# Cross-attention in float32: the tile of batch 0's first softmax sum, and the place of T4's copies on ScalarE in batches 2 to 5

## The chip, the cores and the metric

The kernel runs on one core of a Trainium2 chip. The core has TensorE (PE; its weight loads are listed apart as PEld), VectorE (DVE), ScalarE (ACT), GpSimd (POOL) and SyncE (SP). Each engine executes its own instructions in the order in which the program lists them; semaphores hold an instruction until the ones that it depends on are done. The metric is device time in microseconds. Before the change the median of three runs is 665.91 us (665.89 to 666.24).

## The reference

Eight batches of cross-attention with a residual, all in float32; x1 is `x` and x2 is `ctx_2048`, each 8 x 512 x 1024:

```python
q = jnp.einsum('bcn,dc->bnd', x1, Wq) + bq          # d = 64
k = jnp.einsum('bcn,dc->bdn', x2, Wk) + bk[:, None]
v = jnp.einsum('bcn,dc->bdn', x2, Wv) + bv[:, None]
attn = jax.nn.softmax(jnp.einsum('bnd,bdm->bnm', q, k), axis=2)
attn_out = jnp.einsum('bcm,bnm->bcn', v, attn)
return attn_out + x1
```

## The kernel before

One function, `period`, writes out the work of one batch `s` together with the early work of the next batches `n` and `nn`; it is called for the eight batches in turn, after `head` has begun batch 0. The order of every engine's instructions is the order of the calls in the code; nothing is rescheduled. The framework adds the waits.

**Scores.** For batch `n` the scores are made in two halves `h` of the queries (512 each) and four steps `i`. One step is a pair of score matmuls (L237), which run side by side into two PSUM banks, and two ScalarE copies (L246) into the tile e, one for each bank. In half 0 the banks come from a ring of four that is called `s`, but step 1 takes the two banks `c`. Step 3 of half 0 needs the banks of step 0. Behind the four steps TensorE projects the next batch's queries (L192): in batches 2 to 5 (`s.six`) into the next bank of the ring, which step 2 held; in the others into bank `c0`, which step 1 held. When that is done, SyncE loads the next x tile (L139).

**Softmax.** VectorE folds the maximum and the sum over the steps (`fold`, L258), GpSimd reduces them over the partitions (L274 for the maximum `top`, L306 for the sum `den`), VectorE subtracts the maximum (L342) and ScalarE takes the exponential (L351). `invert` sends the 512 reciprocals to a row in DRAM (L321), and `spread` reads it back onto all partitions (L327). The division comes later, on the product.

**Products.** x2 times the exponentials is computed before Wv is applied. Both are 2 x 2 block products by a seven-product scheme (Strassen's kind); most of the seven are split once more by the same scheme, into inner steps. The names are those of the scheme: product 6 multiplies `S2` and `T2`, product 4 multiplies a block with `T4`, and T4 = T2 - e21, where e21 is one block of the exponentials. `copy_t4` makes -e21 on ScalarE in two parts (L380, 128 x 1024 each), and `add_t4` has two GpSimd DMAs add T2 to it (L386). `multiply_seeded` runs the inner steps of one product in the order 1, 7, 6, 2, 5, 4, 3. Steps 1, 7, 6, 5 and 4 end in ScalarE copies (L858): step 7's goes into a tile v, the "third part", and the others into a bank of the product. Step 6 goes on in the bank `chain` that step 1 wrote, so it waits for step 1's copy. A hook can be hung behind a step.

**Batch 0** multiplies product 6 plainly (`parts_6`, L428) and copies it to the tile u6 on ScalarE (L441), just before the scores of batch 1. Its product 5 has its third part in a tile of the tag `r`.

**Tiles.** Tiles with the same tag share one piece of SBUF (here one buffer for each of `u6`, `r` and `eT4`). Whoever writes a new tile of a tag first waits until all readers of the tile before it are done. The sum of batch 0, half 0, is a tile of tag `u6`: it is folded on VectorE and reduced on GpSimd (L306), and after that u6 holds product 6. The two tags hold tiles of one size. T4's buffer holds, before T4, sums of product 2's inner steps.

Of the kernel before, what the change touches and what calls it, by code (L numbers as in the profile page):

```python
# [15 lines left out]
def kernel(  # L16
# [234 lines left out]
    def fold(s, h, i, kind, op):  # L251

        e = s.e[h]
        if i == 1:
            tag = "u6" if (kind, s.b, h) == ("sum", 0, 0) else "fold"
            s.mx[h] = sb.tile([P, 2, H], F32, tag=tag, name=f"{kind}_{s.b}_{h}")
        f = s.mx[h]
        nc.vector.tensor_tensor(f, e[:, :, 0, :] if i == 1 else f, e[:, :, i, :], op)  # L258

    def folds(s, h, kind, op, to=MH):  # L260

        for i in range(1, to):
            fold(s, h, i, kind, op)
            yield
# [109 lines left out]
    def copy_t4(s, parts=(0, 2)):  # L374

        if parts[0] == 0:
            s.t["T4"] = sb.tile([P, MH, H], F32, tag="eT4", name=f"eT4_{s.b}")
        t4 = s.t["T4"]
        for i in parts:
            nc.scalar.mul(t4[:, i : i + 2, :], s.t["21"][:, i : i + 2, :], -1.0)  # L380

    def add_t4(s):

        t4 = s.t["T4"]
        for i in (0, 2):
            nc.gpsimd.dma_start(t4[:, i : i + 2, :], s.t["T2"][:, i : i + 2, :], accum_op=ALU.add)  # L386
# [225 lines left out]
    def inner_product(s, i, z, ps, opens, *copies):  # L612

        ka, kb, _, _ = MULT[z]
        n_k = s.inner[i][ka].shape[1]
        for k in range(n_k):
            nc.tensor.matmul(  # L617
                ps,
                s.inner[i][ka][:, k, :],
                s.inner[i, "t"][kb][:, k, :],  # L620
                start=opens and k == 0,
                stop=z in (2, 3, 4) and k == n_k - 1,
                skip_group_check=True,
            )
        for copy in copies:
            nc.scalar.copy(copy, ps)

    def inner_parts(s, i):

        ks = ("third", "chain") if i in ((1, 6, 7) if s.six else (2, 7)) else ("chain", "third")  # L630
        of = {k: ps_s.tile([P, H], F32, tag="s", name=f"ps_i{i}{k}_{s.b}")[:, left] for k in ks}
        return of["chain"], of["third"]
# [202 lines left out]
    def multiply_seeded(s, i, v_tag, hooks={}, bank=None):  # L835

        bank = bank or MULT[i][2]

        def fresh(j):
            s.bank[bank, j] = ps = ps_a.tile(  # L840
                [P, H], F32, tag=f"{bank}{j}", name=f"ps_y{bank}{j}_{s.b}_{i}"
            )
            return ps

        b0 = fresh(0)
        chain, third = inner_parts(s, i)
        if v_tag == "top" or s.b == B - 1 and v_tag == "r":
            v = sb.tile([P, H], F32, tag="top", name=f"v{i}_{s.b}", bufs=2)[:, left]
        else:
            v = sb.tile([P, 2, H], F32, tag=v_tag, name=f"v{i}_{s.b}")[:, 0, left]  # L850
        seeded = s.six and i == 5
        if seeded:
            nc.scalar.copy(third, s.v6)

        def step(z, ps, opens, out=None, of=None):
            inner_product(s, i, z, ps, opens)
            if out is not None:
                nc.scalar.copy(out, of)  # L858
            if z in hooks:
                hooks[z]()  # L860

        step(1, chain, True, b0[:, left], chain)
        step(7, third, not seeded, v, third)
        if s.six and i == 6:
            s.v6 = v
        b1 = fresh(1)
        step(6, chain, False, b1[:, left], chain)
        step(2, b0[:, left], False)
        step(5, chain, False, b0[:, right], chain)
        step(4, b1[:, left], False, b1[:, right], chain)  # L870
        step(3, b0[:, right], False)

        def complete(b1=b1):
            b = b1.rearrange("p (a n) -> p a n", a=2)
            nc.vector.tensor_tensor(b, b, v.unsqueeze(1).to_broadcast([P, 2, H // 2]), ALU.add)

        return complete
# [211 lines left out]
    def sums(s, h):  # L1089
        for i in range(1, MH):  # L1090
            fold(s, h, i, "sum", ALU.add)
        total(s, h)
# [34 lines left out]
    def head(s):  # L1127
# [68 lines left out]
        for copy in copies:  # L1196
            copy()
        fold(s, 0, 1, "sum", ALU.add)
        fold(s, 0, 2, "sum", ALU.add)
        fold(s, 1, 1, "max", ALU.max)  # L1200
# [28 lines left out]
    def period(s, n, nn, nnn):  # L1229
# [4 lines left out]
        def first(i, rows=range(2)):  # L1234
            multiply(s, "y", i, s.a, s.t, MH, rows=rows)
# [119 lines left out]
        else:  # L1355
# [51 lines left out]
            if early:  # L1407
                invert(s, 0)
            if s.six:
                multiply_seeded(s, 6, "top", {6: lambda: copy_t4(s, (0,)), 4: lambda: copy_t4(s, (2,))})  # L1410
            else:
                if n:
                    copy_t4(s)
                    add_t4(s)
                first(6)
# [293 lines left out]
    with tc.manual_schedule():  # L1709
        head(states[0])  # L1710
        for b in range(B):
            period(*states[b : b + 4])
# [36 lines left out]
```

## Time and profile before

| | before |
|---|---|
| median of the runs | 665.91 us (665.89 to 666.24) |
| the profiled execution: its time / its span | 665.95 us / 664.2 us |
| TensorE busy | 658.2 us (99%) |
| weight loads busy | 437.4 us (66%) |
| VectorE busy | 622.9 us (94%) |
| ScalarE busy | 387.2 us (58%) |
| GpSimd busy | 215.5 us (32%) |
| granted TensorE clock | 1.0 |

The span is the time from the first to the last instruction of the program, and rows of the timeline give the start within the span, the duration, the engine, the line, the operation, out<-in, the shape and the count. A bracket at the end is idle time of that engine before the row, and what ended it. Where the wait was for several things, the profile names the one that it takes to have come last; if that one was done long before, it was another. A TensorE row's duration overlaps the next row's; distances between starts tell the pace. Float32 matmuls show as two records each. A busy TensorE is not one at its peak.

### The profile page before, as it was taken

The numbers are of one execution on the slowest core, as the hardware profiler recorded it, in microseconds if no ns is written. First come the engines' busy times: TensorE is split into PE (matmuls) and PEld (weight loads), VectorE is DVE, ScalarE is ACT, GpSimd is POOL, SyncE is SP. The second block draws the span as 40 slices with busy tenths as digits, with TensorE's granted clock in tenths as the row PEclk, the third lists the DMA queues.
The fourth block names the chain that finished last, engine by engine and source line by source line (L and its number), as shares of the span: only waits on it lengthen the run. The fifth ranks groups of instructions, "written<-read, shape, count | busy, mean of one in ns | idle before, by whom it ended". The sixth has DMA issues, their size and how long they took to land.

```text
span 664.2 us, 8111 instructions
## 1 busy us (share of the span) xinstructions
PE 658.2 (99%) x2644; PEld 437.4 (66%) x2644; DVE 622.9 (94%) x900; ACT 387.2 (58%) x744; POOL 215.5 (32%) x187
## 2 busy tenths in 40 slices
PE   9999999999999999999999999999999999999997
PEld 4434755757658666787667686676865757656865
DVE  1999999989999998999989999999989999999996
ACT  3754457546495666755667646766567456474332
POOL 0126115531237302282033820346212640224300
PEclk9999999999999999999999999999999999999999
DMA  8697578994789958999699996999957995368614
GB/s 334 252 269 242 139 242 151 215 250 157 234 177 218 244 189 283 175 191 255 183 283 186 191 270 191 250 204 183 292 145 141 207 207 175 76 130 181 121 41 150
DMA packets 48522, 133.26 MB, mean 201 GB/s; under 512 B 5600, under 2 KB 6112, under 8 KB 48480
## 3 DMA queue, kind: packets, MB, share of 16 engines
q0 software_dynamic: 21488, 59.32, 49.1%
q1 hardware_dynamic: 26848, 73.29, 30.5%
q8 instruction: 21, 0.34, 0.2%
q14 instruction: 21, 0.17, 0.1%
q10 hardware_dynamic: 144, 0.14, 0.1%
HBM read 87.83 MB, written 16.81 MB: 158 GB/s over the span
## 4 chain that ended last, share of the span: by engine, by line
PE 84%; DVE 10%; ACT 2%; DMA 1%; issue 1%; POOL 1%; SPq 0%; DVEq 0%
PE ps_yc L617 9%; PE ps_ya L617 7%; PE ps_oc L504 7%; PE ps_s L237 4%; PE ps_oa L504 4%; PE ps_q L192 3%; PE ps_i5chain L617 3%; PE ps_i7chain L617 3%; PE ps_k L192 3%; PE ps_ya L504 3%; PE ps_oa L801 3%; PE ps_i4b L952 3%; PE ps_i3chain L617 3%; PE ps_i1chain L617 3%; PE ps_i2chain L617 3%; PE ps_oc L952 2%
## 5 line engine op out<-in xcount | busy, mean ns | idle before, releaser
L342 DVE TENSOR_TENSOR e<-e,top 128x1024 f32<-128x1024 f32 x60 | 72.2, 1219 | 0.2 <-POOL top L274 0.2
L351 ACT ACTIVATE e<-e 128x1024 f32<-128x1024 f32 x60 | 62.9, 1061 | 15.6 <-DVE e L342 15.3
L274 POOL PARTITION_ALL_REDUCE top<-max x16 | 32.1, 2009 | 110.6 <-DVE max L268 51.7
L246 ACT COPY e<-ps_s 128x512 f32<-128x512 f32 x90 | 47.8, 623 | 9.7 <-PE ps_s L237 7.1
L237 PE MATMUL ps_s<-q,k 64*128 64x512 f32 (+1 forms) x188 | 47.4, 599 | 0.2 <-ACT e L246 0.2
L306 POOL PARTITION_ALL_REDUCE den<-sum x10 | 33.2, 3316 | 31.6 <-DVE sum L268 31.6
L258 DVE TENSOR_TENSOR max<-max,e 128x1024 f32<-128x1024 f32 x30 | 36.6, 1221 | 0.3
L237 PEld LDWEIGHTS ps_s<-q,k 64*128 64x128 f32 x188 | 17.6, 186 | 20.7 <-issue 16.5
L987 DVE TENSOR_TENSOR y<-y,den 128x1024 f32<-128x1024 f32 x24 | 29.3, 1223 | 0.3
L858 ACT COPY ps_yc<-ps_i7chain 128x256 f32<-128x256 f32 x32 | 11.4, 357 | 28.9 <-PE ps_i7chain L617 15.2
L569 DVE TENSOR_TENSOR aI<-a 128x256 f32<-128x256 f32 x60 | 26.8, 447 | 0.0
L287 POOL PARTITION_ALL_REDUCE den<-sum x6 | 19.4, 3230 | 22.0 <-DVE sum L268 22.0
L192 PE MATMUL ps_q<-x_in_x_dram,wqk_sb 128*64 128x512 f32 x112 | 25.6, 598 | 0.4
L327 POOL DMA_DIRECT2D den<-row x12 | 6.7, 560 | 57.8 <-DMA row<-few 42.7
L504 PE MATMUL ps_oc<-yT,w 128*128 128x512 f32 x56 | 25.3, 594 | 0.2 <-DVE uo L1051 0.2
L504 PE MATMUL ps_oa<-yT,w_S 128*128 128x512 f32 x56 | 25.2, 593 | 0.0
L858 ACT COPY ps_ya<-ps_i5chain 128x256 f32<-128x256 f32 x32 | 11.5, 361 | 21.6 <-PE ps_i5chain L617 17.3
L617 PE MATMUL ps_yc<-e,aI 128*128 128x256 f32 x92 | 23.6, 379 | 0.0
L258 DVE TENSOR_TENSOR max<-e 128x1024 f32<-128x1024 f32 x15 | 18.3, 1220 | 5.0 <-POOL den L306 3.1
L858 ACT COPY ps_ya<-ps_i1chain 128x256 f32<-128x256 f32 x28 | 10.0, 357 | 22.1 <-PE ps_i1chain L617 17.0
L170 POOL DMA_DIRECT2D aS<-in_x2T_dram x7 | 6.3, 897 | 50.1 <-ACT aS L166 50.1
L858 ACT COPY ps_yc<-ps_i3chain 128x256 f32<-128x256 f32 x32 | 11.4, 357 | 18.4 <-PE ps_i3chain L617 14.2
(395 smaller groups left out, 1913.8 us busy)
## 6 DMA issues: line engine op xcount, KB each, us to landing
x_in_x_dram<-in_x_dram SPq DMA_DIRECT2D x60, 512.0 KB, 7.7
a<-in_x2T_dram SPq DMA_DIRECT2D x32, 512.0 KB, 8.1
eT<-eT POOLq DMA_DIRECT2D x24, 512.0 KB, 8.4
aS<-in_x2T_dram POOLq DMA_DIRECT2D x21, 512.0 KB, 5.6
uo<-in_x_dram POOLq DMA_DIRECT2D x17, 512.0 KB, 10.7
e<-e POOLq DMA_DIRECT2D x13, 512.0 KB, 7.5
r<-in_x_dram POOLq DMA_DIRECT2D x11, 512.0 KB, 6.8
out_dram<-r SPq DMA_DIRECT2D x11, 512.0 KB, 3.7
```

The source lines that it names most:

```text
L192: nc.tensor.matmul(ps[r, :], w_sb[:, c, :], s.x[:, c, ts(h, H)], start=(c == 0), stop=(c == CT - 1),)
L237: nc.tensor.matmul(ps[g][:, n], s.k[r, ts(i, P)], s.q[r, ts(h, H)][:, n], start=True, stop=True)
L246: nc.scalar.copy(e[:, g, i, :], ps[g])
L258: nc.vector.tensor_tensor(f, e[:, :, 0, :] if i == 1 else f, e[:, :, i, :], op)
L274: nc.gpsimd.partition_all_reduce(s.top[h], s.mx[h][:, 0, :], P, ReduceOp.max)
L306: nc.gpsimd.partition_all_reduce(s.den[h], s.mx[h][:, 0, :], P, ReduceOp.add)
L342: nc.vector.tensor_tensor(e, e, top, ALU.subtract)
L351: nc.scalar.activation(e, e, AF.Exp)
L504: nc.tensor.matmul(ps, left[ka][:, k, ts(j, P)], right[kb][:, k, :], start=opens and k == 0, stop=i in (2, 3, 4) and k == n_k - 1, skip_gr ...
L617: nc.tensor.matmul(ps, s.inner[i][ka][:, k, :], s.inner[i, "t"][kb][:, k, :], start=opens and k == 0, stop=z in (2, 3, 4) and k == n_k - 1 ...
L858: nc.scalar.copy(out, of)
L952: nc.tensor.matmul(ps, s.inner[i][ka][:, k, :], s.inner[i, "t"][kb][:, k, :], start=opens and k == 0, stop=z in (2, 3, 4) and k == n_k - 1 ...
```

## The change

Two independent edits.

In `fold`, the sum of batch 0, half 0, takes the tag `r` instead of `u6`. In `period`, for batches 2 to 5, the first part of T4's copy is issued ahead of product 6 instead of behind its inner step 6, and the second part behind inner step 6 instead of behind step 4.

```diff
@@ fold
         if i == 1:
-            tag = "u6" if (kind, s.b, h) == ("sum", 0, 0) else "fold"
+            tag = "r" if (kind, s.b, h) == ("sum", 0, 0) else "fold"
             s.mx[h] = sb.tile([P, 2, H], F32, tag=tag, name=f"{kind}_{s.b}_{h}")
@@ period
             if s.six:
-                multiply_seeded(s, 6, "top", {6: lambda: copy_t4(s, (0,)), 4: lambda: copy_t4(s, (2,))})
+                copy_t4(s, (0,))
+                multiply_seeded(s, 6, "top", {6: lambda: copy_t4(s, (2,))})
```

The first edit moves no instruction; it changes what some wait for. ScalarE in batch 0, from T4's copies to the scores of batch 1 (`uy_0` is u6 with product 6, `e_0_405` the scores; `PE_49`, `Pool_49` and `DVE_49` are the engines' semaphores; - before, + after):

```order
 L380 ACTIVATE eT_0_327<-e_0_148 128x1024 x2
 L455 ACTIVATE k_359<-ps_k_358,wqk_sb 128x512 [waits PE_49]
-L441 COPY uy_0_378<-ps_ya_0_1_266 128x512 [waits PE_49,Pool_49]
+L441 COPY uy_0_378<-ps_ya_0_1_266 128x512 [waits PE_49]
 L441 COPY uy_0_378<-ps_ya_0_1_274 128x512 [waits PE_49]
-L246 COPY e_0_405<-ps_s_1_0_0_406 128x512 [waits PE_49]
+L246 COPY e_0_405<-ps_s_1_0_0_406 128x512 [waits DVE_49,PE_49]
 L246 COPY e_0_405<-ps_s_1_0_0_407 128x512 [waits PE_49]
 L246 COPY e_0_405<-ps_sc_1_0_1_412 128x512 [waits PE_49]
```

The product's first copy no longer waits for GpSimd; the first score copy now has a wait on VectorE of its own, for the last fold of the sum (L258). The wait on GpSimd goes to the copy of product 5's third part, the tile `v_0` of tag `r`, on ScalarE further on in batch 0:

```order
 L209 ACTIVATE q_439<-ps_q_430,wqk_sb 64x512
 L858 COPY ps_ya_0_5_463<-ps_i5chain_464 128x256 [waits PE_49,Activation_49]
-L858 COPY v_0_466<-ps_i5third_465 128x256 [waits PE_49]
+L858 COPY v_0_466<-ps_i5third_465 128x256 [waits PE_49,Pool_49]
 L858 COPY ps_ya_0_5_473<-ps_i5chain_464 128x256 [waits PE_49,Activation_49]
 L858 COPY ps_ya_0_5_463<-ps_i5chain_464 128x256 [waits PE_49]
```

Nothing else stands between them in another order. The second edit moves two rows on ScalarE. Batch 2, from the last copy of product 1 (L413) to the first score copy of batch 3; `eT` is T4, `ps_i6chain`, `ps_ya` and `v_2` are product 6's. Before:

```order
L413 COPY uy_2_1391<-ps_ya_2_1_1336 128x512
L858 COPY ps_ya_2_6_1414<-ps_i6chain_1416 128x256
L858 COPY v_2_1417<-ps_i6third_1415 128x256
L858 COPY ps_ya_2_6_1424<-ps_i6chain_1416 128x256
L380 ACTIVATE eT_2_1428<-e_0_919 128x1024
L858 COPY ps_ya_2_6_1414<-ps_i6chain_1416 128x256
L858 COPY ps_ya_2_6_1424<-ps_i6chain_1416 128x256
L380 ACTIVATE eT_2_1428<-e_0_919 128x1024
L246 COPY e_0_1451<-ps_s_3_0_0_1452 128x512
```

and after the change:

```order
L413 COPY uy_2_1391<-ps_ya_2_1_1336 128x512
L380 ACTIVATE eT_2_1414<-e_0_919 128x1024
L858 COPY ps_ya_2_6_1416<-ps_i6chain_1418 128x256
L858 COPY v_2_1419<-ps_i6third_1417 128x256
L858 COPY ps_ya_2_6_1426<-ps_i6chain_1418 128x256
L380 ACTIVATE eT_2_1414<-e_0_919 128x1024
L858 COPY ps_ya_2_6_1416<-ps_i6chain_1418 128x256
L858 COPY ps_ya_2_6_1426<-ps_i6chain_1418 128x256
L246 COPY e_0_1451<-ps_s_3_0_0_1452 128x512
```

Each of the two L380 rows stands three or two rows earlier, and nothing follows the last inner copy but the score copies. The first L380 keeps its waits, which are for the T4 transfers of the batch before. The second copy of product 6 to u6 (L408), behind the scores, gets a wait for ScalarE's own last inner copy. Batches 3 to 5 read the same, and the other engines' instructions stay in their order.

## The prediction

> **What bounds the kernel now.** I read the page first, then the chain that ended last, then who waited for whom, and last the timeline at the two edited places.
>
> ```profile
> PE 658.2 (99%) x2644; PEld 437.4 (66%) x2644; DVE 622.9 (94%) x900; ACT 387.2 (58%) x744; POOL 215.5 (32%) x187
> ```
>
> TensorE is busy for 658.2 of 664.2 us, and VectorE for 622.9. So an edit on ScalarE (ACT) or GpSimd (POOL) counts only where TensorE's work starts later because of it. Such a place stands in the chain, in batch 0:
>
> ```profile
> 50.87 3.24 POOL den L306
> 54.13 1.07 ACT uy L441 x2
> ...
> 55.74 1.61 PE ps_s L237 x3
> ```
>
> GpSimd reduces the first softmax sum, ScalarE waits for it to copy product 6 out, and TensorE's scores wait for ScalarE. The waits of ScalarE name the same place, and one that touches the second edit:
>
> ```profile
> ACT uy L441 <- POOL den L306: 4.5, 1, 4.5
> ...
> ACT e L246 <- ACT eT L380: 2.5, 4, 0.6
> ```
>
> The columns are total us, times, longest. The first is part 1 of the change. The second invites the reading that T4's copy (L380) keeps four batches' score copies waiting 0.6 us each; the timeline below decides that.
>
> **Part 1: the sum moves from tile u6 to tile r.** The copies at L441 write u6, which until now held the sum that the reduction L306 reads. With the sum in r, L441 waits only for its own matmuls. The same place before, on TensorE, ScalarE and the weight loads:
>
> ```profile
> 45.65 7.13 PE L428 MATMUL ps_ya<-eT,aS 128*128 128x512 f32 x16
> 52.72 1.13 PE L237 MATMUL ps_s<-q,k 64*128 64x512 f32 x4
> 55.09 1.09 ACT L246 COPY e<-ps_s 128x512 f32<-128x512 f32 x2
> 55.74 0.29 PEld L237 LDWEIGHTS ps_s<-q,k 64*128 64x128 f32 x2 [1.01 <-ACT e L246]
> 57.29 3.65 PE L192 MATMUL ps_q<-x_in_x_dram,wqk_sb 128*64 128x512 f32 x16
> ```
>
> Four pairs of score matmuls start at 52.72, the projection of the next queries at 57.29: 4.57 us. The fourth pair needs the banks of the first, which ScalarE frees late. The same sequence in batch 1, where nothing holds ScalarE:
>
> ```profile
> 135.45 1.13 PE L237 MATMUL ps_s<-q,k 64*128 64x512 f32 x4
> 136.65 1.07 ACT L246 COPY e<-ps_s 128x512 f32<-128x512 f32 x2 [0.51 <-PE ps_s L237]
> 139.08 1.51 PE L192 MATMUL ps_q<-x_in_x_dram,wqk_sb 128*64 128x512 f32 x6
> ```
>
> Here it takes 139.08 - 135.45 = 3.63 us, and the first copy starts 1.20 us after the first score. After the change the last product-6 matmul still ends at 45.65 + 7.13 = 52.78, the second L441 copy (1.07 / 2, about 0.55 us) ends near 53.4, and the first score copy starts at 52.72 + 1.20 = 53.92 in place of 55.09. That is soon enough for the fourth pair to find its banks free, so TensorE gains 4.57 - 3.63 = **0.94 us** at this place. The wait does not vanish: it goes to the copy of product 5's third part into r, at about 62 us, while the reduction ended at 50.87 + 3.24 = 54.11; cost nothing, with 8 us to spare. The first score copy also gets a wait for VectorE's last fold of the sum; in the chain the reduction that reads this sum starts at 50.87, so the fold was over before 52.72. No DMA moves past another.
>
> Does the 0.94 us reach the end? VectorE is not moved by it at first, and then meets two places where it waited for TensorE anyway:
>
> ```profile
> 67.44 1.23 DVE L599 TENSOR_TENSOR eI3eT<-e 128x1024 f32<-128x1024 f32 x1 [0.78 <-PE ps_ya L617]
> 73.00 0.70 DVE L875 TENSOR_TENSOR ps_yc<-ps_yc,v 128x512 f32<-128x512 f32 x1 [0.40 <-ACT ps_yc L858]
> 77.30 0.56 POOL L327 DMA_DIRECT2D den<-row  x1 [10.95 <-DMA row<-few]
> 77.88 1.78 POOL L274 PARTITION_ALL_REDUCE top<-max  x1
> 79.98 0.28 DVE L641 TENSOR_TENSOR w_I<-w,w_I 128x128 f32<-128x128 f32 x1
> 80.18 2.35 DVE L342 TENSOR_TENSOR e<-e,top 128x1024 f32<-128x1024 f32 x2
> ```
>
> It had 0.78 idle before 67.44 and 0.40 before 73.00, together 1.18, so from 73 on it is 0.94 earlier too. What is late next is GpSimd: its maximum (L274) stands behind the issue of L327, which waits for the 2 KB row of reciprocals. If that row lands no earlier, the maximum still ends at 77.88 + 1.78 = 79.66, and VectorE, which subtracts it from 80.18, gains at most 80.18 - 79.66 = 0.52. What the row stands behind:
>
> ```profile
> 60.98 1.75 SPq L139 DMA_DIRECT2D x_in_x_dram<-in_x_dram  x4
> 65.07 1.28 POOL L321 DMA_DIRECT2D row<-few  x1
> 62.00:66.00 4.00, 4.00 (x20) 3.23 (x19) 4.00 (x8) 1.76 (x5) 3.70 (x5) 1.00 0.87 318
> 66.00:70.00 4.00, 4.00 (x20) 3.53 (x19) 3.22 (x7) 1.15 (x4) 0.35 (x1) 1.00 0.92 271
> ```
>
> (The last two are stretches; the number before the last is the DMA engines' busy share.) SyncE's four x loads, issued when the query projection has freed x, fill the engines at 0.87 to 0.92, and GpSimd's two T4 transfers and the row follow. The loads' issue hangs on the projection and moves 0.94 earlier; in a queue this full most of that should reach the row. Bounds: the row moves by 0 or by 0.94. I take 0.94, since the queue is busy throughout. With 0 VectorE lags TensorE by 0.94 - 0.52 = 0.42, and the tightest place behind is
>
> ```profile
> 126.88 2.35 DVE L365 TENSOR_TENSOR eT<-eT,e 128x1024 f32<-128x1024 f32 x2
> 128.49 7.03 PE L504 MATMUL ps_ya<-eT,aS 128*128 128x512 f32 x16
> ```
>
> The first of the two sums ends about 126.88 + 1.2 = 128.1, 0.4 us before product 6 of batch 1 reads it, and the weight loads want it some 0.2 sooner. TensorE would lose 0.2 to 0.4 there, and part 1 would be worth 0.5 to 0.7.
>
> **Part 2: T4's copies one place forward, batches 2 to 5.** Per batch two ScalarE copies of 1.06 us, none added. The first moves from behind product 6's third step to ahead of its first; the second takes its place. In batch 2:
>
> ```profile
> 209.26 0.59 ACT L413 COPY uy<-ps_ya 128x512 f32<-128x512 f32 x1
> 210.77 0.36 ACT L858 COPY ps_ya<-ps_i6chain 128x256 f32<-128x256 f32 x1 [0.92 <-PE ps_i6chain L617]
> 211.18 0.82 PEld L617 LDWEIGHTS ps_i6chain<-eI6y,aI 128*128 128x128 f32 x4
> 212.77 1.06 ACT L380 ACTIVATE eT<-e 128x1024 f32<-128x1024 f32 x1
> 215.30 1.06 ACT L380 ACTIVATE eT<-e 128x1024 f32<-128x1024 f32 x1
> 215.79 1.13 PE L237 MATMUL ps_s<-q,k 64*128 64x512 f32 x4
> 217.00 1.07 ACT L246 COPY e<-ps_s 128x512 f32<-128x512 f32 x2 [0.63 <-ACT eT L380]
> 219.59 0.20 PEld L192 LDWEIGHTS ps_q<-x_in_x_dram,wqk_sb 128*64 128x64 f32 x4 [0.92 <-ACT e L246]
> ```
>
> *What it could gain.* The scores start at 215.79, the query projection at 219.59: 3.80, that is 0.17 over batch 1's 3.63, and 0.68 over four batches. But the second copy of T4 ends at 215.30 + 1.06 = 216.36, while the first score copy starts 217.00 - 215.79 = 1.21 after the first score, against 1.20 in batch 1, where no T4 copy stands ahead of it. So the matmul came last, and the releaser in brackets had long been done. The 0.17 is the projection's bank: here it takes a bank that the fifth score copy frees, and copies run at about 0.5 us each. Gain 0 to 0.17 a batch; I take **0**.
>
> The Trainium skill (Perfetto Trace Analysis, Optimization Strategy) reads a gap that repeats for a stretch as a sign that there may not be enough SBUF or PSUM for the next tile. By it the 0.92 is a bank's price, which no order of T4's copies changes, and part 2 brings 0; by the bracketed releaser it would bring up to 0.68. The offset of 1.21 against 1.20 agrees with the page.
>
> *What it could cost.* ScalarE idles 0.92 before 210.77. T4's copy would start at 209.26 + 0.59 = 209.85 at the latest and end at 210.91, so the chain's copy comes up to 0.14 late, and with it the weight load at 211.18. What a late weight load costs shows in batch 0:
>
> ```profile
> 61.84 1.03 PE L617 MATMUL ps_i5third<-eI5y,aI 128*128 128x256 f32 x4
> 62.81 0.73 PEld L617 LDWEIGHTS ps_i5chain<-eI5u,aI 128*128 128x128 f32 x4 [0.35 <-ACT ps_ya L858]
> 63.78 1.03 PE L617 MATMUL ps_ya<-eT,aS 128*128 128x256 f32 x4
> ...
> 214.14 1.73 PE ps_ya L617 x8
> ```
>
> Eight matmuls took 63.78 - 61.84 = 1.94 with a hold of 0.35, against 1.73 in the chain at 214.14: 0.21. So about 0.14 of a hold is hidden by the weight load's lead, and a delay of 0.14 costs nothing. Bounds 0 to 4 x 0.14 = 0.56; I take **0**. T4's transfers do not start sooner: GpSimd issues them behind other work.
>
> The skill (TensorE: Matmul & The Clock Gate, Step-by-step: what each phase is for) says that weight loads are pulled ahead of running matmuls. By that alone a late copy would cost less than 0.21; in the row the load stands held by the copy, so the row's price is used.
>
> **Sum.** The profiled execution took 665.95 us (span 664.2), 0.04 from the median 665.91. 665.95 - 0.94 - 0 + 0 = **665.0 us**, a gain of 0.14%.
>
> **The rivals.**
>
> *VectorE keeps part of it.* The row lands when it did, the maximum ends at 79.66, and TensorE pays 0.2 to 0.4 back near 128.49. For it: the row's long wait. Against it: the loads ahead of it move. 665.95 - 0.5 = **665.4**; chance 0.22.
>
> *Part 2 pays too.* T4's copy really holds the score copies: 0.94 + 4 x 0.17 = 1.62, **664.3**. For it the bracket, against it the equal offsets; chance 0.08.
>
> *Slower.* T4's first copy holds the chain's copy of product 6 in all four batches. It needs a copy that starts late or runs long: at a hold of 0.38 the price, 0.38 - 0.14 = 0.24 a batch, eats part 1; a hold of 0.7 gives 4 x 0.56 - 0.94 = +1.3, **667.3**. Against it: the 0.92 idle and the 1.06 that both copies took. Chance 0.04.
>
> *The wait stays.* Something else holds the copies at L441 as long: **665.95**. The only matmuls that they read ended at 52.78, which speaks against it; chance 0.04.
>
> **How the numbers follow.** The forecast case has 0.62. A measurement of this kernel tells about 0.2%, 1.33 us, from no change. The forecast, the partial case and the case without effect lie within it; only part 2 paying, and a tail of the forecast, go under 664.6: faster 0.10. Slower by 1.33 needs nearly all of the slower case: 0.03. Same: 0.87. The likeliest case alone spans 664.7 to 665.3; the range reaches to the two neighbours, 664.3 to 666.0, and leaves out the slower case.
>
> **What would show it.** Right: L441 starts near 51 and without GpSimd as its releaser; the first score copy starts near 53.9; the projection starts near 56.35; VectorE's subtraction (L342, 80.18 before) is about 0.9 earlier; all stages from 130 to 550 are earlier by one constant; in batches 2 to 5 scores to projection stay at 3.80. Wrong: that 3.80 falls to 3.63 (part 2 pays), or product 6's weight load shows a hold on ScalarE (part 2 costs), or L342 moves only 0.5 and TensorE waits for L365 near 128 (the partial case).

## The result, and the profile after

| | before | after |
|---|---|---|
| median of 20 runs each | 666.04 us (665.78 to 666.88) | 665.09 us (663.92 to 666.58) |
| the profiled execution: its time / its span | 665.95 / 664.2 us | 665.07 / 663.3 us |
| TensorE busy | 658.2 us | 657.1 us |
| GpSimd busy | 215.5 us | 216.6 us |

The ratio of the times is 0.9984, 95% interval 0.9977 to 0.9991. The forecast was 665.0 us. The gain is real and smaller than the 0.2% taken beforehand as the limit of what can be told apart. What the forecast did not say at all is the spread: the runs of the changed kernel lie 2.7 us apart, those of the kernel before 1.1 (1.3 to 1.9 in the later series). Most of what follows is about that spread, because it shows what the removed wait had covered.

The profile's first line and a stretch of the chain that ended last, both of the changed kernel. The columns of the chain are start, length and what ran:

```profile
PE 657.1 (99%) x2644; PEld 436.9 (66%) x2644; DVE 622.7 (94%) x900; ACT 387.2 (58%) x744; POOL 216.6 (33%) x187
```

```profile
36.02 8.79 DMA x_in_x_dram<-in_x_dram
...
44.86 1.08 PE ps_k L451 x4
45.94 7.06 PE ps_ya L428 x16
53.00 1.06 PE ps_s L237 x4
...
56.63 3.58 PE ps_q L192 x16
```

Before, this stretch of the chain went through GpSimd's L306 and ScalarE's L441 (50.87 and 54.13). Both are gone from it. In their place stands a transfer: the last quarter of batch 1's x, which the keys' product (L451) reads. The timeline of the changed kernel at the same place, TensorE and ScalarE:

```profile
44.86 1.08 PE L451 MATMUL ps_k<-x_in_x_dram,wqk_sb 128*64 128x512 f32 x4 [0.53 <-DMA x_in_x_dram<-in_x_dram]
51.32 0.58 ACT L441 COPY uy<-ps_ya 128x512 f32<-128x512 f32 x1 [1.75 <-PE ps_ya L428]
54.09 1.07 ACT L246 COPY e<-ps_s 128x512 f32<-128x512 f32 x2 [0.47 <-PE ps_s L237]
56.56 3.65 PE L192 MATMUL ps_q<-x_in_x_dram,wqk_sb 128*64 128x512 f32 x16
```

L441 is released by TensorE now, at 51.32 for about 54.1 before. The scores start at 52.93, the first score copy 1.16 us later, and the projection at 56.56: scores to projection takes 56.56 - 52.93 = 3.63 us, 0.94 less than before. But the projection is only 57.29 - 56.56 = 0.73 us earlier, since the scores themselves start 0.21 us later (52.93 for 52.72). The same wait for x stood in the kernel before:

```profile
44.64 1.08 PE L451 MATMUL ps_k<-x_in_x_dram,wqk_sb 128*64 128x512 f32 x4 [0.29 <-DMA x_in_x_dram<-in_x_dram]
```

There x let TensorE go on at 44.64, here at 44.86. That is the 0.21. VectorE and GpSimd later in batch 0, of the changed kernel:

```profile
75.36 0.56 POOL L327 DMA_DIRECT2D den<-row  x1 [8.88 <-DMA row<-few]
76.19 2.75 POOL L274 PARTITION_ALL_REDUCE top<-max  x1 [0.27 <-DVE few L320]
79.46 2.35 DVE L342 TENSOR_TENSOR e<-e,top 128x1024 f32<-128x1024 f32 x2
```

GpSimd could issue L327, which waits for the row of reciprocals, 1.94 us earlier (75.36 for 77.30). The x loads ahead of the row were issued only 0.72 earlier (60.26 for 60.98), but the last of them landed 2.14 earlier (69.20 for 71.34). VectorE's subtraction is 0.72 earlier (79.46 for 80.18), as much as TensorE's 0.73.

Part 2's place in batch 2 of the changed kernel, ScalarE, TensorE and its weight load:

```profile
209.01 1.07 ACT L380 ACTIVATE eT<-e 128x1024 f32<-128x1024 f32 x1
210.05 0.36 ACT L858 COPY ps_ya<-ps_i6chain 128x256 f32<-128x256 f32 x1
215.07 1.13 PE L237 MATMUL ps_s<-q,k 64*128 64x512 f32 x4
216.27 1.07 ACT L246 COPY e<-ps_s 128x512 f32<-128x512 f32 x2 [1.60 <-PE ps_s L237]
218.87 0.20 PEld L192 LDWEIGHTS ps_q<-x_in_x_dram,wqk_sb 128*64 128x64 f32 x4 [0.93 <-ACT e L246]
```

T4's first copy runs from 209.01 in ScalarE's idle time, and product 6's chain copy follows at 210.05, which is 0.72 before its old 210.77, as much as everything else: no hold. Scores to projection is 218.87 - 215.07 = 3.80, as before. The first score copy, 1.20 us after the first score, now names TensorE as its releaser where it named T4's copy, and starts no sooner relative to the scores.

### The profile page after: what moved, and what is told of

Same layout as the page of the kernel before. It is cut to its first block, busy times and chain, and to the rows that moved or that the text cites. A ratio compares the mean times of both kernels' runs of the same rounds, so it can differ in the third digit from the quotient of the medians.

```text
span 663.3 us, 8112 instructions
## 1 busy us (share of the span) xinstructions
PE 657.1 (99%) x2644; PEld 436.9 (66%) x2644; DVE 622.7 (94%) x900; ACT 387.2 (58%) x744; POOL 216.6 (33%) x187
## 4 chain that ended last, share of the span: by engine, by line
PE 89%; DVE 5%; DMA 2%; ACT 2%; SPq 1%; issue 1%
PE ps_yc L617 9%; PE ps_ya L617 7%; PE ps_oc L504 7%; PE ps_s L237 5%; PE ps_ya L504 4%; PE ps_q L192 4%; PE ps_oa L504 4%; PE ps_i5chain L617 3%; PE ps_i7chain L617 3%; PE ps_k L192 3%; PE ps_oa L801 3%; PE ps_i4b L952 3%; PE ps_i1chain L617 3%; PE ps_i3chain L617 3%; PE ps_i2chain L617 3%; PE ps_oc L952 2%
## 5 line engine op out<-in xcount | busy, mean ns | idle before, releaser
L342 DVE TENSOR_TENSOR e<-e,top 128x1024 f32<-128x1024 f32 x60 | 72.1, 1217 | 0.2 <-POOL top L274 0.2
L306 POOL PARTITION_ALL_REDUCE den<-sum x10 | 33.3, 3333 | 31.7 <-DVE sum L268 26.8
L258 DVE TENSOR_TENSOR max<-max,e 128x1024 f32<-128x1024 f32 x30 | 36.5, 1218 | 0.3
L569 DVE TENSOR_TENSOR aI<-a 128x256 f32<-128x256 f32 x60 | 24.7, 411 | 0.0
L327 POOL DMA_DIRECT2D den<-row x12 | 6.7, 560 | 53.5 <-DMA row<-few 38.3
L258 DVE TENSOR_TENSOR max<-e 128x1024 f32<-128x1024 f32 x15 | 18.3, 1218 | 4.3 <-POOL den L306 3.1
L192 PE MATMUL ps_k<-x_in_x_dram,wqk_sb 128*64 128x512 f32 x96 | 21.9, 598 | 0.0
```

The lines of the kernel that those rows point to most:

```text
L192: nc.tensor.matmul(ps[r, :], w_sb[:, c, :], s.x[:, c, ts(h, H)], start=(c == 0), stop=(c == CT - 1),)
L306: nc.gpsimd.partition_all_reduce(s.den[h], s.mx[h][:, 0, :], P, ReduceOp.add)
L342: nc.vector.tensor_tensor(e, e, top, ALU.subtract)
```

## The experiments

The kernel before was timed anew beside each series of experiments (medians 666.09 to 666.14 us). The changed kernel was not; its 665.09 us comes from the runs of the result. A difference of 0.2 us from it is within the noise.

**Each part alone.** Two kernels, each with one of the two edits.

```diff
 part 1 alone, in fold; T4's copies stay in their old places
-            tag = "u6" if (kind, s.b, h) == ("sum", 0, 0) else "fold"
+            tag = "r" if (kind, s.b, h) == ("sum", 0, 0) else "fold"
 part 2 alone, in period; the sum stays in u6
-                multiply_seeded(s, 6, "top", {6: lambda: copy_t4(s, (0,)), 4: lambda: copy_t4(s, (2,))})
+                copy_t4(s, (0,))
+                multiply_seeded(s, 6, "top", {6: lambda: copy_t4(s, (2,))})
```

> Part 1 alone: the first sum of batch 0 in tile r, T4's first copy of batches 2 to 5 left in its old place. Theory (all of the change's gain is part 1's): 665.1 us, 0.9 to 1.0 under the kernel before, and in the profile scores to projection in batch 0 at 3.63 us. It also has the wider spread of the changed kernel, about 2.5 us between its runs, if that spread comes from part 1. Rival (part 2 carries some of it): 665.4 to 665.9.

> Part 2 alone: T4's first copy of batches 2 to 5 ahead of product 6, the first sum of batch 0 left in tile u6. Theory (part 2 is worth nothing and costs nothing): 666.0 us, within 0.2 of the kernel before, batch 0's copies at L441 again released by GpSimd's L306, and runs as close together as those of the kernel before, about 1 us. Rival (part 2 carries some of the gain): 665.1 to 665.7. Second rival (the wider spread is part 2's): 666.0 with runs spread over 2.5 us.

Part 1 alone: 665.33 us (664.05 to 666.83), ratio 0.9986 (0.9977 to 0.9995). Part 2 alone: 665.97 us (665.56 to 666.34), ratio 0.9997 (0.9988 to 1.0005). Part 1's time cannot be told from the changed kernel's, and part 2's interval leaves out the gain. So the gain and the spread are both part 1's, and part 2 is worth nothing that these runs can tell. The profiled execution of part 1 alone happened to be a long one, 666.60 us, and shows where a long one is long. Its timeline, TensorE:

```profile
46.15 1.08 PE L451 MATMUL ps_k<-x_in_x_dram,wqk_sb 128*64 128x512 f32 x4 [0.35 <-DMA x_in_x_dram<-in_x_dram]
54.22 1.13 PE L237 MATMUL ps_s<-q,k 64*128 64x512 f32 x4
57.86 3.65 PE L192 MATMUL ps_q<-x_in_x_dram,wqk_sb 128*64 128x512 f32 x16
```

The last quarter of x came 1.29 us later than in the changed kernel's profile (46.15 for 44.86), and the projection 1.30 later (57.86 for 56.56). Scores to projection is 3.64. This gave the theory for the runs that follow: **the wait for GpSimd had covered the landing of x, and with it gone each execution ends as late as its own transfer did.** The rival: the place has slack, and the spread comes from elsewhere.

**TensorE waits for x with other work in hand.** In batch 0 the keys' fourth step is put behind two of product 6's part products, 1.7 us later. The same edit was made on the kernel before.

```diff
-            more_keys(0, 1, 2, 3)
-            load_x(nn, x1)
+            more_keys(0, 1, 2)
             parts_6(s, 0)
+            more_keys(3)
+            load_x(nn, x1)
+            parts_6(s, 1)
             parts_6(s, 2)
 # parts_6(s, 0) now does the products of k = 0 alone, parts_6(s, 1) those of k = 1
```

> The changed kernel, and in batch 0 the fourth tile of the keys' product (L451), which waits for the last quarter of x (DMA landing at 44.81 us, PE idle 0.53 us), is issued after the first two of product 6's eight part products, 1.7 us later on PE. Theory (with GpSimd's wait gone the landing of that load is on the path, in full, and its variation too): the idle of 0.53 us before L451 goes, the scores start 0.5 us earlier, time 664.5 us (0.5 to 0.7 under the changed kernel), and the runs are closer together, about 1 us between lowest and highest. Rival (the wait is followed by slack, and the spread comes from elsewhere): 665.1 us, spread still 2.5 us.

> The same shift of the keys' fourth tile, on the kernel before. Theory (there the copies at L441 wait for GpSimd's L306, which does not depend on that tile, so the landing of x is hidden under that wait): 666.0 us, no gain, though PE's idle before L451 goes. Rival (PE's idle is on the path in either kernel): 665.6 to 665.7, by the 0.29 us idle in its profile.

On the changed kernel: 664.88 us (664.34 to 665.11), ratio 0.9981 (0.9972 to 0.9989). The runs are 0.8 us apart where they were 2.7, as the theory had it. The 0.5 us of gain did not come; the medians differ by 0.2, which the intervals do not tell from nothing. The timeline of TensorE in that kernel:

```profile
46.08 1.08 PE L450 MATMUL ps_k<-x_in_x_dram,wqk_sb 128*64 128x512 f32 x4
52.44 1.13 PE L237 MATMUL ps_s<-q,k 64*128 64x512 f32 x4
59.05 1.08 PE L192 MATMUL ps_q<-x_in_x_dram,wqk_sb 128*64 128x512 f32 x4 [0.19 <-DMA x_in_x_dram<-in_x_dram]
```

The wait at the keys is gone and the scores start 0.49 earlier (52.44 for 52.93). Then the projection's last four wait for x again. All x tiles share one buffer, so the next load goes out only when the keys' fourth step has read the old one: at 47.20 instead of 45.98, and its last quarter landed at 59.01 instead of 56.90. The stall went to the next transfer, and the 0.4 us was given back there.

On the kernel before: 666.25 us (665.54 to 666.80), ratio 1.0002 (0.9993 to 1.0010), no gain, though TensorE's wait at the keys is gone there too. Its timeline:

```profile
55.64 1.61 PE L237 MATMUL ps_s<-q,k 64*128 64x512 f32 x4 [0.34 <-ACT e L246]
57.18 3.65 PE L192 MATMUL ps_q<-x_in_x_dram,wqk_sb 128*64 128x512 f32 x16
```

The scores began early (52.45) and waited for ScalarE, which had waited for GpSimd. The projection starts at 57.18, as in every profile with the sum in u6 (57.1 to 57.3, table below).

**Two ways to make x later that did not.** First, the load was issued behind the two writes of q.

```diff
         evict = queries(n)
-        load_x(n, x2)
         evict()
+        load_x(n, x2)
         highest(s, 1)
```

> The changed kernel, with SyncE issuing batch 1's x for the keys behind the two writes of q in batch 0 (L213) instead of ahead of them, so that the four issues leave about 2 us later (near 36.6 to 38.1 us for 34.6 to 36.0). Theory (the landing of that load sets the scores of batch 0 in the changed kernel): the last quarter lands near 46.8 to 47.3 us for 44.8, the scores and all behind them move by as much, time 667.1 to 667.6 us. Rival (the load has slack): under 665.6 us.

> The same later load, on the kernel before. Theory (the first 0.94 us of its lateness is hidden under the copies' wait for GpSimd's L306, the rest is not): the same end as the changed kernel with the later load, 667.1 to 667.6 us, 1.1 to 1.6 over the kernel before, so that the change is then worth nothing. Rival (the landing counts in full in either kernel, and the change's gain is kept): 668.1 to 668.6 us.

On the changed kernel: 665.28 us (664.88 to 666.40); on the kernel before: 665.86 us (665.55 to 666.08). Neither expectation held, since the landing did not move. The chain of the first:

```profile
38.37 6.52 DMA x_in_x_dram<-in_x_dram
...
44.93 1.08 PE ps_k L451 x4
```

The last quarter was issued 2.35 us later (38.37 for 36.02) and landed at 44.89 for 44.81: its transfer took 6.52 us for 8.79. The writes of q, which had shared the DMA engines with it and landed at 45.30 and 45.85, now landed ahead of it, at 38.68 and 39.22. From 34 to 44 us the DMA engines are busy all the time in every one of these kernels (share 0.93 to 1.02), and in these two executions the later issue did not land later. Why is argued, not shown: the two writes went ahead of the load instead of beside it. As tests of a later landing the two runs say nothing.

Second, a transfer of 512 KB that nobody reads was put ahead of the load on SyncE's queue.

```diff
         evict = queries(n)
+        nc.sync.dma_start(dram.tile([P, N], F32, name="unused"), x2[n.b, 0:P, :])
         load_x(n, x2)
```

> The changed kernel, with one transfer more on SyncE's queue, ahead of batch 1's x for the keys in batch 0: 512 KB of x2 from DRAM to a place in DRAM that nobody reads. The quarters of x land 1.2 to 1.4 us apart when nothing else shares the queues (39.33, 40.64, 42.09 us), so the last one should land at least that much later. Theory (the landing sets batch 0's scores in the changed kernel): PE's wait ahead of L451's last four, and the time, grow by what the landing moves, 1.2 us or more: 666.3 us or more. Rival (the landing is not on the path): 665.1 us.

> The same added transfer, on the kernel before. Theory (up to 0.94 us of a later landing is hidden under the copies' wait for GpSimd's L306): if the landing moves by 1.25 us, only about 0.3 us of it shows, 666.4 us; whatever it moves by, the end is within 0.2 us of the changed kernel's with the same transfer once it is over 0.94. Rival (the landing counts in full in either kernel, so the change keeps its gain): 0.9 us over the changed kernel with the same transfer, 667.2 us or more.

On the changed kernel: 664.73 us (664.13 to 666.23); on the kernel before: 666.29 us (665.56 to 667.01). This edit missed its mark too. SyncE's timeline shows why:

```profile
21.89 0.61 SPq L1209 DMA_DIRECT2D unused<-in_x_dram  x1
34.41 1.91 SPq L139 DMA_DIRECT2D x_in_x_dram<-in_x_dram  x4
```

The transfer waits for nothing, so it went out at 21.89, behind the load before, and was long over at 34.41 (it landed at 29.96). The two profiles are still of use, because x happened to land at other times in them. On the changed kernel it landed at 43.95, just as TensorE came to it, and the execution took 664.13 us. The timeline of TensorE:

```profile
41.37 3.70 PE L451 MATMUL ps_k<-x_in_x_dram,wqk_sb 128*64 128x512 f32 x16
55.70 3.65 PE L192 MATMUL ps_q<-x_in_x_dram,wqk_sb 128*64 128x512 f32 x16
```

The keys take 3.70 us, where they take 3.65 without any wait (last experiment below). On the kernel before x landed at 45.28:

```profile
45.32 1.08 PE L451 MATMUL ps_k<-x_in_x_dram,wqk_sb 128*64 128x512 f32 x4 [0.66 <-DMA x_in_x_dram<-in_x_dram]
57.12 3.65 PE L192 MATMUL ps_q<-x_in_x_dram,wqk_sb 128*64 128x512 f32 x16
```

That is 0.68 later than in the profile of before (45.32 for 44.64), and the projection is no later: 57.12 for 57.29.

**The last quarter loaded twice.** Here the added bytes cannot run ahead, since they go into the tile that TensorE still reads.

```diff
     def load_x(s, x, twice=False):
+        if twice:                      # for batch 1's x2, in head_second
+            nc.sync.dma_start(s.x[:, 3, :], x[s.b, ts(3, P), :])
         for c in range(CT):
             nc.sync.dma_start(s.x[:, c, :], x[s.b, ts(c, P), :])
```

> The changed kernel, with the fourth quarter of batch 1's x for the keys loaded twice: once ahead of the other three and once in its place, the same bytes into the same tile, so that 512 KB more lie ahead of the landing that PE waits for and none of it can go before PE has left the tile. The second transfer cannot be issued before the first has landed, near 39.3 us. Theory (that landing sets batch 0's scores): the last quarter lands at 46.0 us or later for 44.8, the first scores start 1.2 us later or more, and the time grows by as much: 666.3 us or more, as late as the kernel before or later. Rival (the landing is not on the path, and the spread of the changed kernel has another source): 665.1 us.

666.33 us (665.30 to 669.50), ratio 1.0008 (0.9997 to 1.0019). The chain of this kernel (its lines stand two further down):

```profile
35.71 4.79 DMA x_in_x_dram<-in_x_dram
...
40.51 6.76 DMA x_in_x_dram<-in_x_dram
...
47.32 1.08 PE ps_k L453 x4
...
59.10 3.58 PE ps_q L194 x16
```

The last quarter landed at 47.27, 2.46 later than in the changed kernel's profile; the projection starts at 59.03, 2.47 later. Not all of that is the edit's. The first transfer of this load was already issued 1.14 later (35.71 for 34.57), because TensorE had waited longer for the first loads of the kernel:

```profile
6.96 1.94 PE L1106 MATMUL ps_q<-x_head,wqk_sb 128*64 128x512 f32 x8 [0.39 <-DMA x_head<-in_x1h_dram]
```

That leaves 2.46 - 1.14 = 1.32 for the added bytes, and the median is 1.24 over the changed kernel's (666.33 for 665.09). By the medians the whole gain of the change is gone (666.33 for 666.10). The theory holds.

The profiled executions together, ordered by the landing of that quarter (all by the trace, in us). The two with the keys' fourth step moved are left out, since other work stands in the path there. A kernel with the sum in r no longer waits for GpSimd at L441; one with the sum in u6 does.

| kernel | sum in | landing | projection starts | landing + 11.75 | time |
|---|---|---|---|---|---|
| x in two tiles (below) | r | 43.30 | 55.79 | 55.05 | 663.62 |
| unread transfer, changed | r | 43.95 | 55.70 | 55.70 | 664.13 |
| changed | r | 44.81 | 56.56 | 56.56 | 665.07 |
| load behind q, changed | r | 44.89 | 56.64 | 56.64 | 665.35 |
| T4's copy twice (below) | r | 45.10 | 56.85 | 56.85 | 670.27 |
| part 1 alone | r | 46.10 | 57.86 | 57.85 | 666.60 |
| bank (below) | r | 46.61 | 58.36 | 58.36 | 666.21 |
| last quarter twice | r | 47.27 | 59.03 | 59.02 | 667.44 |
| part 2 alone | u6 | 43.36 | 57.17 | 55.11 | 666.01 |
| load behind q, before | u6 | 44.27 | 57.09 | 56.02 | 665.99 |
| before | u6 | 44.60 | 57.29 | 56.35 | 665.95 |
| unread transfer, before | u6 | 45.28 | 57.12 | 57.03 | 666.46 |

With the sum in r the projection follows the landing at a constant distance of 11.75 us; for a landing before about 43.95 TensorE no longer waits, and 55.7 to 55.8 is the least. With the sum in u6 it starts at 57.1 to 57.3 at every landing seen, 43.36 to 45.28. So at the projection the change is worth about 57.2 - 55.7 = 1.5 us in an execution whose x lands early and 0.94 where it lands at 44.60. It should be worth nothing from about 57.2 - 11.75 = 45.4 on; no profile with the sum in u6 has so late a landing.

The start of the projection decides the time: in the five rows with the sum in r whose edits change nothing behind it (unread transfer, changed, load behind q, part 1 alone, last quarter twice), the execution takes 608.4 to 608.7 us more than that start. With the sum in u6 it is 608.7 to 609.3. Two smaller sources of spread show beside the landing. The first is the kernel's first loads, as in the run above: TensorE reaches the keys at 41.4 to 41.6 in most profiles, but at 41.82 (load behind q, changed), 42.19 (bank) and 42.66 (last quarter twice). The second is VectorE in batch 1, at the place that the prediction's first rival named. In part 1 alone, VectorE and the weight load of product 6:

```profile
127.90 2.35 DVE L365 TENSOR_TENSOR eT<-eT,e 128x1024 f32<-128x1024 f32 x2
129.18 0.30 PEld L504 LDWEIGHTS ps_ya<-eT,aS 128*128 128x128 f32 x2 [0.37 <-ACT ps_yc L858]
```

The first of the two sums ends at about 129.1, and the weight load starts right behind it; the copy in the bracket was done at 128.75. TensorE loses 0.23 us there. Seven of the fourteen profiles, with the sum in r and in u6, lose 0.1 to 0.7 us there or in product 2 just before, where a copy on ScalarE waits for VectorE's L1051; those of before and of the changed kernel lose nothing.

Why the landing varies so between executions is open: in the profiles of part 1 alone and part 2 alone the last quarter was issued at 35.90 and 35.94, and landed at 46.10 and 43.36. The rate of the DMA engines from 34 to 44 us varies at full load. Two stretches, of part 2 alone (landing at 43.36) and of the bank's run (issued at 36.69, landing at 46.61); the last two columns are the DMA engines' busy share and GB/s:

```profile
34.00:44.00 10.00, 10.00 (x32) 3.87 (x30) 9.69 (x11) 4.54 (x5) 2.68 (x1) 1.00 1.02 322
```

```profile
34.00:44.00 10.00, 10.00 (x30) 3.59 (x26) 9.66 (x11) 4.54 (x5) 2.68 (x1) 1.00 0.97 269
```

The rate goes along with the landing only roughly (the changed kernel: 297 GB/s and 44.81; part 1 alone: 289 and 46.10), and what sets it was not tried.

**The price of a copy that holds the chain.** The prediction's slower rival put a price on it; T4's first copy was made twice.

```diff
                 copy_t4(s, (0,))
+                nc.scalar.mul(s.t["T4"][:, 0:2, :], s.t["21"][:, 0:2, :], -1.0)
                 multiply_seeded(s, 6, "top", {6: lambda: copy_t4(s, (2,))})
```

> The changed kernel, with T4's first copy made twice ahead of product 6 in batches 2 to 5 (one more L380 of 1.0 us on ScalarE, the same values written again). The prediction's price for a first copy that holds product 6's chain copy was the hold less 0.14 us in each of four batches. Theory (that price): the chain copy at L858 starts 0.95 to 1.0 us later, PE waits 0.8 to 0.85 us a batch more, 3.3 us in all, 668.4 us. Rival (product 6 has other work to fill the hold): within 0.5 us of the changed kernel, 665.1 to 665.6.

669.30 us (669.13 to 670.27), ratio 1.0048 (1.0035 to 1.0062): 4.2 us over the changed kernel's median, 0.9 more than expected. The timeline in batch 2:

```profile
210.78 1.06 ACT L1411 ACTIVATE eT<-e 128x1024 f32<-128x1024 f32 x1
211.75 0.37 ACT L858 COPY ps_ya<-ps_i6chain 128x256 f32<-128x256 f32 x1
212.17 1.13 PE L617 MATMUL ps_i6chain<-eI6y,aI 128*128 128x256 f32 x4 [0.68 <-ACT ps_ya L858]
```

Batch 2 starts 0.67 us later here than in the changed kernel's profile (x landed 0.29 later, and 0.38 more were lost near 124 to 129 in batch 1, the place named above). Beyond that the chain copy is 211.75 - 210.05 - 0.67 = 1.03 late, and TensorE falls 0.94 behind in each of batches 2 to 5. So the cover was 0.09 us, not the 0.14 of the prediction. Another 0.18 us a batch is lost at product 3, where a ScalarE copy into ps_yc starts about 0.28 us after its matmuls allow. The kernel before shows that late copy once, in batch 2; the changed kernel not at all. ScalarE in batch 2, before and then after:

```profile
236.76 0.36 ACT L858 COPY ps_yc<-ps_i3chain 128x256 f32<-128x256 f32 x1 [1.70 <-PE ps_i3chain L617]
```

```profile
235.76 0.36 ACT L858 COPY ps_yc<-ps_i3chain 128x256 f32<-128x256 f32 x1 [1.43 <-PE ps_i3chain L617]
```

That is 1.00 us apart, where everything just ahead is 0.72 apart. In the run with T4's copy twice, 4 x (0.94 + 0.18) + 0.67 = 5.15 is nearly the whole distance of the two profiles (670.27 - 665.07 = 5.20). What makes that copy late stays open.

The Trainium skill (TensorE: Matmul & The Clock Gate, Step-by-step: what each phase is for) says that weight loads are pulled ahead of running matmuls. Here TensorE lost 0.94 of a hold of 1.03; no run shows whether the other 0.09 is due to that.

**The bank.** The prediction put the 0.17 us by which batches 2 to 5 exceed 3.63 down to the bank that the projection takes. Now the third row of scores, instead of the second, goes to the separate bank.

```diff
-            then = scores_and(n, 0, 1, "c", next_queries if nn else nothing)
+            then = scores_and(n, 0, 2 if s.six else 1, "c", next_queries if nn else nothing)
```

> The changed kernel, and in batches 2 to 5 it is the third row of the next batch's scores, and no longer the second, that goes to the bank of its own (ps_sc). The projection's bank is then freed by the third score copy instead of the fifth. In the profile of the changed kernel the projection's weight load waits 0.93 us for that fifth copy, and scores to projection takes 3.80 us where batch 0 has 3.63. Theory (the 0.17 us between the two is the price of that bank): 3.63 us in batches 2 to 5 too, 0.68 us in all, 664.4 us. Rival (the rows merely change places, and another row waits as long): 665.1 us.

664.27 us (663.54 to 666.21), ratio 0.9972 (0.9963 to 0.9981), 0.82 under the changed kernel's median. The timeline of TensorE in batch 2:

```profile
216.86 1.99 PE L237 MATMUL ps_s<-q,k 64*128 64x512 f32 x8
220.50 3.65 PE L192 MATMUL ps_q<-x_in_x_dram,wqk_sb 128*64 128x512 f32 x16
```

220.50 - 216.86 = 3.64, and this profile gains 0.16 to 0.17 on the changed kernel's at each of the four places. The 0.17 was the bank's price. The Trainium skill (Perfetto Trace Analysis, Optimization Strategy) takes a gap that repeats as a hint at too little SBUF or PSUM, and this run agrees in that the gap was a bank's wait: another use of the same banks, with none added, took 0.66 us off that the new order of T4's copies had not touched. The spread stays at 2.7 us, as it should where the landing of x is still in the path.

**A version that beats both.** The bank, and x in two tiles of two quarters each: the first half of the next load goes out as soon as TensorE has read the first half of the old one.

```diff
-        s.x = sb.tile([P, CT, N], F32, tag="x", name=f"x_{s.b}_{x.tensor.name}")
+        s.x = x_tiles(f"x_{s.b}_{x.tensor.name}")
...
+    def x_tiles(name):   # Halves picks the tile of a quarter
+        return Halves(*(sb.tile([P, 2, N], F32, tag=f"x{i}", name=f"{name}_{i}") for i in range(2)))
```

> The changed kernel, with the third row of scores in the bank of its own (as in the run on that bank), and with x in two tiles of two quarters each instead of one tile, so that the first half of the next load is issued as soon as PE has read the first half, some 1.7 us earlier. Theory (the last quarter then lands before PE wants it at 44.3 us): PE's idle ahead of L451's last four goes, 663.7 us, runs within 1.2 us. Rival (the transfers are bound by the bytes queued ahead, as with the later issue, where the landing did not move either): 664.3 us, spread 2.5 us.

663.90 us (663.51 to 664.11, 5 runs), ratio 0.9965 (0.9953 to 0.9978): 2.2 us under the kernel before in the same runs. The timeline of TensorE (lines stand 14 further down):

```profile
41.51 3.65 PE L465 MATMUL ps_k<-x_in_x_dram,wqk_sb 128*64 128x512 f32 x16
55.79 3.65 PE L206 MATMUL ps_q<-x_in_x_dram,wqk_sb 128*64 128x512 f32 x16
```

The keys run through in one piece. The first half was issued at 32.84 instead of 34.57, the last quarter landed at 43.30, the next one at 52.96 (56.90 in the changed kernel), and the runs lie 0.6 us apart. One early landing would prove little, since landings vary; the narrow runs are the evidence that the transfers are out of the path, and they are only five. The two tiles without the bank were not run.

## Why the prediction was right, and where it was not

*Part 1, 0.94 us.* Right in mechanism and, in the profile, in size: L441 started at 51.32 with TensorE as its releaser, scores to projection took 3.63 us, the copy of product 5's third part was released by TensorE (62.23). The working left out one thing. It kept the start of the scores at 52.72, the row of one execution, and took the 4.57 - 3.63 from there. That start hangs on TensorE's wait for x at L451, which in the kernel before was hidden under the wait for GpSimd and afterwards is not. The step that asked what is late next looked behind the edit, at the row of reciprocals, and not ahead of it. So 0.94 was the gain at one landing, 44.60; over executions it is 0 to 1.5 by the table. In the profiled pair x landed 0.21 later afterwards, and 0.73 was left at the projection. That the median came out right to 0.1 us is partly luck: the one profile of before happened to have a landing that is neither early nor late (43.3 to 47.3 in the table).

*Does it reach the end.* Yes. The row came early, VectorE's L342 moved 0.72 as TensorE did, and TensorE lost nothing near 128. In this pair the rival in which VectorE keeps part of it did not come true. But the place that it named is a real one: half of the profiles lose 0.1 to 0.7 us there or just before, and what makes VectorE late in them was not followed. "One constant from 130 to 550" was nearly right: 0.72 up to batch 2 (scores at 215.07 for 215.79), then 0.90 (batch 5's at 455.37 for 456.27), because the kernel before had its one late copy at product 3 in between. The working does not have that 0.18, and without it these two profiles would be 0.7 apart instead of 0.88; that their distance comes near 0.94 is luck. Four of the five profiles with the sum in u6 show it there, and none with the sum in r but the one with T4's copy twice; whether it comes with part 1 is open.

*Part 2, gain 0.* Right: 3.80 in the profile, 665.97 us alone. The releaser that the profile named, T4's copy, had long been done, and the equal offsets of 1.21 and 1.20 said so. Part 2 alone does not rule out a gain below 0.8 us, the end of its interval; the profile's 3.80 does. The bank's run shows where the 0.17 lay.

*Part 2, cost 0.* Right: the chain copy at 210.05 moved with everything else. The margin was thinner than the text made it. T4's copy starts at 209.01 and takes 1.07, so it frees ScalarE just as the chain copy's matmuls end; one more copy of about 1 us cost 0.94 at once, plus 0.18 further on. The slower rival was priced a little too low and did not come true.

*The range and the chances.* 664.3 to 666.0 holds the median, but not all single runs. No case of the prediction spoke of executions that differ.

## What to carry to other kernels

When an edit removes the wait that ends last, look for waits ahead of it on the same path that it made harmless, not only for what is late behind it: a short wait for a DMA (here 0.29 us, on a busy engine, in no chain) becomes the bound, and its run-to-run variation shows in full. A wider spread after a gain can be a sign of that, and more room for the transfer (a load in halves, work put in the wait) took it away here. Where a stall is moved by reordering, see which buffer is freed later for it: the next load in the same buffer takes the stall over.

## What was not expected of the hardware

The same transfer, issued at 35.9 us, landed at 43.36 in one execution and at 46.10 in another, with the DMA engines full in both. Issuing a load 2.35 us later behind two short writes did not move its landing (44.89 for 44.81); no run shows why. And a ScalarE copy started about 0.28 us late at product 3 in one batch of the kernel before and in all four of the kernel with T4's copy made twice, with nothing in the profile to say why.
